# A four-layer graph network on one core: the first layernorm in halves ahead of the adjacency, first tokens over two bank pairs, four units added to x on VectorE, and new due times throughout

## Chip, core and metric

The kernel runs on one core of one Trainium2 chip. The metric is the device time of one execution in microseconds. The time before is the median of three runs, 2805.03 us (2801.18 to 2805.45). A core has five engines with queues of their own: TensorE (PE, with PEld for its weight loads), VectorE (DVE), ScalarE (ACT), GpSimd (POOL) and SyncE (SP), which only issues DMAs. Each engine runs its instructions in the order in which they stand.

## What is computed

Eight samples of 2048 nodes with 128 features pass through four layers, each a layernorm, a relu, graph attention over one adjacency matrix that all share, and an addition to x. Layers 0, 1 and 3 are attention with additive scores (one head); layer 2 has four heads with dot products as scores.

```python
def _L1_gnn_ref(h, adj, W, a):              # layer 0: the same, then elu; layer 3: a second layernorm, residual, elu
    Wh = jnp.einsum('bnf,fo->bno', h, W)
    a_src, a_dst = (a[:F_out], a[F_out:])
    s_src = jnp.einsum('bnf,f->bn', Wh, a_src)
    s_dst = jnp.einsum('bnf,f->bn', Wh, a_dst)
    e = jax.nn.leaky_relu(s_src[:, :, None] + s_dst[:, None, :], negative_slope=LEAKY_SLOPE)
    masked = jnp.where(adj[None, :, :] > 0, e, NEG_BIG)
    attention = jax.nn.softmax(masked, axis=-1)
    return jnp.einsum('bij,bjf->bif', attention, Wh)

def _L2_gnn_ref(input_tensor, adj_matrix):
    x = input_tensor.reshape(B, S, H, F // H)
    scores = jnp.einsum('bihk,bjhk->bhij', x, x)
    scores = jax.nn.leaky_relu(scores, negative_slope=ALPHA)
    scores = jnp.where(adj_matrix[None, None, :, :] == 0, -jnp.inf, scores)
    probs = jax.nn.softmax(scores, axis=-1)
    out = jnp.einsum('bhij,bjhk->bihk', probs, x)
    return out.reshape(B, S, F)

for each layer k:
    h = jnp.maximum(_layernorm(x, axis=-1), 0.0)
    x = x + layer_k(h, adj)
```

## The kernel before

The adjacency is loaded in 16 blocks of 128 rows and turned once into a byte mask, `edge`, that stays in SBUF (`adjacency`, L365). Its symmetry is tested on PE (`symmetry`, L378 and L382), and a slower general path exists for the case that a test fails.

A *unit* is one layer of one sample. The three additive layers are `Gat` units. Their beginning is the layernorm (statistics L448, six small operations L100 to L105, a power on GpSimd L110, L115), the rows of h on ScalarE (L476), and, for each of four quarters, transposes (L504), a copy (L522), the projection (L530), exponentials (L559 to L561) and the rows y (L555). The factors r of all targets are spread over the partitions by PE in three units (L614, L621) and through a row in DRAM in the others. Then come the *tokens*: 32 for a unit, 16 source blocks for each half of the targets. A token is one VectorE operation over 128x1024 (L653, `zg`) and eight matmuls on PE (L662), which the profile shows as 16. When a half is complete its sums are divided (L694, L695), passed through elu where the layer has it, and added to x. In layers 0 and 1 that addition is an accumulating DMA from GpSimd (`plus_a`, L730).

Layer 2 is a `Heads` unit. Its h goes to DRAM in two parts (halves, L803), and is loaded again in other shapes (L817, L823, L828). For each head 16 *beats* follow: four score matmuls on PE (L878), two exponentials on ScalarE (L885), one mask on VectorE (L891) and the weighing with the values on PE (L900). A head ends with a copy, transposes, a division (L920) and an accumulating DMA that adds its columns to x (`gather`, L925).

PSUM has eight banks. `pair` is the name of bank pairs that transposes, projections, scores and the symmetry test take in turn; tokens of place 0 sum in banks 1 to 3. In the first unit alone both halves run together, and place 1 sums in banks 0, 6 and 7, so that only one pair, 4 and 5, is free until that unit ends.

The order of every engine is made while the program is built. `add` records an operation with its engine, an assumed duration, a due time, what it needs, the slots it takes and frees, and `Plan.run` places the operations one after another: of those on an engine that can start within `WINDOW_US` of the first, the one with the lowest due time goes first. The due times come from tables (`TOKENS`, `BEATS`, `LEADS`: start and step by unit) and from `EARLY`, an offset by kind of operation. `order` is then emitted as it stands. The engines' program is fixed by this; on the chip each instruction waits for its inputs alone.

Of the kernel before, what the change touches and what calls it, by code (L numbers as in the profile page):

```python
# [8 lines left out]
F32 = mybir.dt.float32  # L9
# [11 lines left out]
P = 128  # L21
HEADS = 4
# [18 lines left out]
def adj_preln_d4(ctx: ExitStack, tc: tile.TileContext, x, adj, w0, a0, w1, a1, w3, a3,  # L41
# [53 lines left out]
    def moments_begin(stat, name, st):  # L95


        var = stat.tile([P, 4, NB], F32, tag="var", name=f"var{name}")
        total, apart, square, v = (var[:, k, :] for k in range(4))
        nc.vector.tensor_sub(apart, st[:, :, 1], st[:, :, 4])  # L100
        nc.vector.tensor_add(v, st[:, :, 2], st[:, :, 5])
        nc.vector.tensor_add(total, st[:, :, 1], st[:, :, 4])
        nc.vector.scalar_tensor_tensor(square, apart, 0.25, apart, op0=OP.mult, op1=OP.mult)
        nc.vector.tensor_scalar(v, v, 1.0 / C, EPS, op0=OP.mult, op1=OP.add)
        nc.vector.tensor_add(v, v, square)  # L105
        return total, v
# [51 lines left out]
    HURRY_US, WINDOW_US, BEAT_SUMS_US = 372.0, 0.136, 0.86  # L158

    EARLY = dict(front=-36.6, score=230.5, exp=53.6, mask=-103.3, sums=-160.7)  # L160

    SINGLY = (7,)
    PLUS_US, PLUS_LAG_US, GATHER_US, GATHER_LAG_US = 1.0, 5.5, 2.2, 6.5
# [73 lines left out]
    def fast(ctx):  # L237
# [9 lines left out]
        SUMS = ((1, 2, 3), (0, 6, 7))  # L247
        plan = Plan(dict(pair=(4,), sums=(0,), more=(1,), low=0, z=5, zg=3, r=2, h=3, h_t=2, hi=1, lo=1,
# [24 lines left out]
        def load_weights(op):  # L273
# [4 lines left out]
            load(out=a0_sb, in_=a0.rearrange("o (t p) -> p (o t)", p=P))  # L278
            load = nc.gpsimd.dma_start
# [76 lines left out]
        def adjacency(j):  # L356
# [10 lines left out]
            last = add("SP", 2.7, 0.1 * j, load, takes=[tag], lag=3.0)  # L367
            rows_in.append(add("DVE", 1.14, 40.0 + 3.5 * j, edges, [last], frees=[(tag, last)]))

        def symmetry(j):  # L370

            wide = (j + 1) * P
            for k in range(0, wide, 512):
# [12 lines left out]
                due = 130.0 + 9.0 * j  # L386
                last = add("PE", 0.1 + 0.1 * w / P, due, differences, [rows_in[j]], takes=["pair"])
# [23 lines left out]
        def load_x(b, due):  # L411
            def load(op):
                X[b] = big.tile([P, NB, C], F32, tag="x", name="x", bufs=4)
                xv = x[b].rearrange("(n p) c -> p n c", p=P)
                for q in range(4 if b == 0 else 1):
                    sl = slice(q * 4, q * 4 + 4) if b == 0 else slice(0, NB)
                    nc.sync.dma_start(out=X[b][:, sl, :], in_=xv[:, sl, :])

            x_taken[b] = add("SP", 1.5, due, load, takes=["x"], lag=17.0 if b else 5.0)
# [4 lines left out]
        class Unit:  # L424
# [15 lines left out]
            def moments(self, name, part, rows, needs):  # L440
# [17 lines left out]

                last = []
# [5 lines left out]
                return key, add("DVE", 0.09, self.due(part + 0.14), end, last)  # L465

            def rows_made(self, part, step):

                key, last = self.moments("x", 0.0, lambda: X[self.b], [self.after] * 4)
                out = []  # L470
# [14 lines left out]
                for q in range(4):  # L485
                    takes, before = ["h"], []
                    if q == 0 and self.layer != 2:
                        takes, before = ["h", "y"], y_takers[-1:]
                    first = last = add("ACT", 1.54, self.due(part + step * q), lambda op, q=q: rows(op, q),
                                       [last] + before, takes=takes)  # L490
# [18 lines left out]
        class Gat(Unit):  # L509
# [62 lines left out]
            def second(self, ends):  # L572

                key, last = self.moments("h", 0.6, lambda: self.y[:, :, :C], [[e] for e in ends])
# [27 lines left out]
            def spread(self):  # L602
# [4 lines left out]
                if (self.b, self.layer) in ((0, 0), (0, 1), (B - 1, 3)):  # L607
                    for half in range(2):
# [7 lines left out]
                        turned = add("PE", 0.9, self.due(0.95), turn, last, takes=["pair", "r"])  # L616
# [10 lines left out]
                def write(op):  # L627
                    self.row = dram.tile([N], F32, name="row", bufs=4)
                    nc.sync.dma_start(out=self.row.rearrange("(n p) -> p n", p=P), in_=self.cr[:, 1, :])

                self.written = add("SP", 0.5, self.due(0.82 if self.layer == 3 else 0.9), write, last, lag=11.5)

            def targets(self, half, due):
# [10 lines left out]
                self.r_ready[half] = op, op  # L644

            def token(self, a, due, place, last_front, last_back, first, last, gate=None):
# [11 lines left out]
                def back(op):  # L658
                    z = self.z.pop(a)
                    for i in range(HB):  # L660
                        k = i % 3
                        nc.tensor.matmul(ps[:, SUMS[place][i // 3], k * CE:(k + 1) * CE],  # L662
# [9 lines left out]
                        takes=[name] if first else [], frees=[("zg", f)])  # L672
# [9 lines left out]
            def out(self, half, back, place, name, due):  # L682
# [4 lines left out]
                def divided(op):  # L687
# [3 lines left out]
                    for g in range(3):  # L691
                        i0, i1 = g * 3, min(g * 3 + 3, HB)
                        pv = ps[:, SUMS[place][g], :(i1 - i0) * CE].rearrange("p (k c) -> p k c", c=CE)
# [38 lines left out]
                last = taker = add("DVE", 1.75, due - 30, divided, [back], takes=["oa"])  # L732
                last.frees.extend([("pair", 6), ("low", 0)] if place else [(name, self.sums_taker[half])])
                if layer == 1:
                    done.setdefault((b, layer + 1), []).append(
                        add("POOL", PLUS_US, due + 6, plus_a, [last], frees=[("oa", taker)], lag=PLUS_LAG_US))
# [4 lines left out]
                else:  # L741
# [7 lines left out]
                    for k in range(3):  # L749
# [3 lines left out]
                late = due + (10 if layer == 0 else 22)  # L753
                e = add("DVE", 1.14, late, elu_e, [e], frees=[("oe", e_taker)])
                if layer == 0:
                    done.setdefault((b, layer + 1), []).append(
                        add("POOL", PLUS_US, late + 4, plus_a, [last, e], frees=[("oa", taker)], lag=PLUS_LAG_US))
# [12 lines left out]
        class Heads(Unit):  # L770
# [133 lines left out]
            def finish(self, h, weigh, low, due):  # L904
# [19 lines left out]
                def gather(op):  # L924
# [6 lines left out]
                done.setdefault((self.b, 3), []).append(  # L931
                    add("POOL", GATHER_US, due + 5, gather, [last], frees=[("o", turned)], lag=GATHER_LAG_US))
# [6 lines left out]
            (1, 0, 0): (82.8, 3.82), (0, 1, 0): (298.0, 0.56), (0, 1, 1): (-1.8, 0.58),  # L939
            (1, 0, 1): (237.5, 5.12), (2, 0, 0): (716.8, 6.16), (2, 0, 1): (906.2, 4.64),  # L940
            (1, 1, 0): (732.2, 3.64), (1, 1, 1): (825.9, 6.82), (3, 0, 0): (663.1, 5.57),
            (3, 0, 1): (930.0, 5.2), (2, 1, 0): (1062.7, 6.76), (2, 1, 1): (705.4, 6.0),
            (0, 3, 0): (1035.8, 5.99), (0, 3, 1): (1142.1, 4.99), (3, 1, 0): (1367.5, 5.63),
            (4, 0, 0): (905.1, 4.26), (4, 0, 1): (912.9, 5.97), (3, 1, 1): (1359.7, 0.0),
            (1, 3, 0): (1117.7, 6.03), (1, 3, 1): (796.7, 5.75), (4, 1, 0): (778.4, 5.37),
            (4, 1, 1): (1685.2, 3.89), (5, 0, 0): (1293.2, 5.84), (5, 0, 1): (1766.2, 6.15),
            (2, 3, 0): (2097.3, 7.1), (2, 3, 1): (1822.4, 6.83), (5, 1, 0): (1860.6, 4.87),
            (5, 1, 1): (1480.8, 7.43), (3, 3, 0): (1598.7, 4.59), (6, 0, 0): (1737.4, 5.35),
            (6, 0, 1): (2113.6, 6.85), (3, 3, 1): (2672.7, 4.26), (6, 1, 0): (2603.6, 7.7),
            (6, 1, 1): (2772.8, 1.33), (7, 0, 0): (2564.1, 4.71), (7, 0, 1): (2932.1, 6.8),  # L950
            (4, 3, 0): (2517.6, 5.02), (7, 1, 0): (2277.6, 0.32), (7, 1, 1): (2588.8, 7.43),
            (4, 3, 1): (2924.9, 6.32), (5, 3, 0): (2998.9, 5.51), (6, 3, 0): (2609.9, 6.67),
            (5, 3, 1): (2731.2, 7.57), (6, 3, 1): (3009.1, 7.1), (7, 3, 0): (2581.0, 4.89),
            (7, 3, 1): (3032.4, 0.56),
        }
        BEATS = {
            (0, 0): (65.79, 11.57), (0, 1): (-149.43, 13.67), (0, 2): (460.38, 2.51),
            (0, 3): (521.27, 3.93), (1, 0): (151.07, 16.02), (1, 1): (505.63, 8.12),
            (1, 2): (398.27, 6.65), (1, 3): (632.45, 4.8), (2, 0): (616.54, 11.88),
            (2, 1): (827.83, 6.13), (2, 2): (917.3, 2.2), (2, 3): (1137.58, 12.88),  # L960
            (3, 0): (505.03, 9.63), (3, 1): (796.86, 5.93), (3, 2): (1050.45, 2.24),
            (3, 3): (1141.98, 8.73), (4, 0): (1335.0, 23.07), (4, 1): (1518.23, 6.15),
            (4, 2): (1530.27, 6.19), (4, 3): (1810.32, 4.9), (5, 0): (1553.66, 11.16),
            (5, 1): (2021.07, 3.65), (5, 2): (2225.85, 7.65), (5, 3): (2286.21, 0.76),
            (6, 0): (2061.58, 5.82), (6, 1): (2080.76, 0.07), (6, 2): (2097.15, 0.0),
            (6, 3): (2106.74, 13.2), (7, 0): (1522.48, 2.92), (7, 1): (1574.93, 6.28),
            (7, 2): (1813.8, 4.07), (7, 3): (2104.58, 1.02),
        }
        LEADS = {
            (0, 0): 190.15, (1, 0): 14.27, (0, 1): 346.94, (2, 0): 414.97, (1, 1): 500.75,  # L970
            (3, 0): 386.01, (2, 1): 340.86, (0, 3): 529.94, (3, 1): 136.87, (4, 0): 509.55,
            (1, 3): 1755.37, (4, 1): 701.37, (5, 0): 419.44, (2, 3): 1032.06, (5, 1): 76.28,
            (6, 0): 565.92, (3, 3): 513.74, (6, 1): 369.01, (7, 0): 403.81, (4, 3): 213.24,
            (7, 1): 525.14, (5, 3): 302.24, (6, 3): 846.56, (7, 3): 88.27, (0, 2): 390.41,
            (1, 2): 712.99, (2, 2): 419.3, (3, 2): -281.82, (4, 2): -699.34, (5, 2): 257.63,
            (6, 2): -206.25, (7, 2): -140.03,
        }

        def planned():
            weights = add("ACT", 1.0, 0.0, load_weights, lag=4.0)  # L980
            projected[0] = projections(0, 9.0, [weights])
            units[0, 0] = Gat(0, 0, 10.0, 40.0)
            for j in range(NB):
                adjacency(j)
            more = add("POOL", 5.0, 26.0, load_more, lag=4.0)
            projected[1] = projections(1, 50.0, [weights, projected[0]])
# [5 lines left out]
            for n in range(2 * NB):  # L992
                f, b = units[0, 0].token(n % 2 * NB + n // 2, 45.0 + 2.4 * n, n % 2, f, b, n < 2, n >= 2 * NB - 2)
# [231 lines left out]
```

## Time and profile before

| what | us |
|---|---|
| median of three runs | 2805.03 |
| the profiled execution, whole | 2799.68 |
| its span, first to last instruction | 2797.9 |
| PE busy | 2642.8 (94%) |
| VectorE busy | 2510.4 (90%) |
| ScalarE busy | 1713.5 (61%) |
| GpSimd busy | 259.1 (9%) |

The span is the time from the first to the last instruction of the profiled execution; the execution itself took 1.8 us more. "Busy" is time in which an engine works on at least one instruction. A matmul's end is modelled, so PE that is busy may also be waiting within its pipeline. The granted clock is given for PE alone, as a share of full speed; over the whole execution it was 0.989. In a timeline a row has the start, the time from the first to the last of the merged instructions, engine, line, operation, tiles out<-in with their size, the count, and in brackets the engine's idle time before it and what ended it.

### The profile page before, as it was taken

Reading aid. Unit: us, or ns where it says so; the run is one execution under the profiler, and the core shown is the slowest. Engines: PE = TensorE matmul, PEld = TensorE weight load, DVE = VectorE, ACT = ScalarE, POOL = GpSimd, SP = SyncE. Lnnn points to the kernel's source line nnn. Section 1 sums busy time; section 2 is a strip of 40 time slices with the busy share of each in tenths; the row PEclk is TensorE's granted clock in tenths of the full one; section 3 lists DMA queues with packets and bytes.
Section 4 is the critical chain, followed back from the end, with each engine's and each line's share of the span. In section 5 each row is a group of like instructions: output and inputs, shape, how many; then the busy total and the mean of one; then the engine's idle time right before and its main releaser. Section 6 shows DMA issues by size and latency. Waiting matters only on the chain. (4 is left out here: it accounts for less than half of the span.)

```text
span 2797.9 us, 48899 instructions
## 1 busy us (share of the span) xinstructions
PE 2642.8 (94%) x20083; PEld 2030.7 (73%) x20083; DVE 2510.4 (90%) x3309; ACT 1713.5 (61%) x2767; POOL 259.1 (9%) x120
## 2 busy tenths in 40 slices
PE   5999999999998999998999999999999999898987
PEld 4989787767774778886767777765787677564687
DVE  5766799989999999998989998999899999999987
ACT  3432465666668558555667756567676757788541
POOL 1100000002000102000100110000000100001010
PEclk9999999999999999999999999999999999999999
DMA  8003523162134312523232344323226231522010
GB/s 306 24 16 58 102 54 63 43 115 47 49 74 102 56 47 47 96 68 61 49 77 39 61 90 84 61 46 83 46 57 106 46 65 34 110 55 53 12 20 25
DMA packets 258442, 185.20 MB, mean 66 GB/s; under 512 B 187616, under 2 KB 222560, under 8 KB 252064
## 3 DMA queue, kind: packets, MB, share of 16 engines
q1 hardware_dynamic: 186784, 156.46, 23.1%
q0 software_dynamic: 71008, 25.45, 8.7%
q8 instruction: 159, 2.61, 0.4%
q14 instruction: 75, 0.61, 0.1%
q10 hardware_dynamic: 416, 0.07, 0.0%
HBM read 123.03 MB, written 33.73 MB: 56 GB/s over the span
## 5 line engine op out<-in xcount | busy, mean ns | idle before, releaser
L885 ACT ACTIVATE z<-ps,shift 128x1024 f32<-128x1024 f32 x1024 | 1119.4, 1114 | 720.8 <-PE ps L878 709.8
L662 PEld LDWEIGHTS ps<-y,zg 128*128 128x128 f32 x12288 | 1471.0, 193 | 82.8 <-DVE zg L653 29.2
L662 PE MATMUL ps<-y,zg 128*128 128x129 f32 x12288 | 1502.8, 277 | 23.2 <-DVE zg L653 17.3
L891 DVE SCALAR_TENSOR_TENSOR z<-z,edge 128x2048 f32<-128x2048 f32 x512 | 1168.7, 2286 | 73.7 <-ACT z L885 72.5
L653 DVE SCALAR_TENSOR_TENSOR zg<-r,cr,edge 128x1024 f32<-128x1024 f32 x768 | 972.1, 1279 | 113.3 <-PE ps L662 101.7
L878 PE MATMUL ps<-m,s 128*128 128x512 f32 x2048 | 718.9, 437 | 70.7 <-ACT z L885 64.5
L878 PEld LDWEIGHTS ps<-m,s 128*128 128x128 f32 x2048 | 314.4, 191 | 348.6 <-ACT z L885 254.3
L900 PE MATMUL ps<-z,v 128*32 128x512 f32 x4096 | 503.7, 604 | 8.2 <-DVE z L891 8.1
L900 PEld LDWEIGHTS ps<-z,v 128*32 128x32 f32 x4096 | 103.7, 109 | 239.0 <-issue 182.7
L476 ACT ACTIVATE h<-x,nmrx,rstdx 128x128 f32<-128x128 f32 x512 | 210.5, 491 | 53.2 <-DVE nmrx L115 41.1
L110 POOL TENSOR_TENSOR rstdx<-varx,neg_half 128x16 f32<-128x16 f32 x32 | 124.3, 3885 | 644.6 <-DVE varx L105 544.6
L925 POOL DMA_DIRECT2D x<-o x32 | 67.9, 2122 | 785.4 <-DVE o L920 746.7
L448 DVE BATCH_NORM_STATS2 st<-x 128x6 f32<-128x128 f32 x512 | 109.5, 279 | 6.7 <-DMA x<-o 6.7
L530 PEld LDWEIGHTS ps<-rhs,h_t 128*128 128x128 f32 x768 | 100.0, 196 | 15.8 <-ACT h_t L522 7.9
L530 PE MATMUL ps<-rhs,h_t 128*128 128x130 f32 x768 | 106.8, 284 | 4.7 <-ACT h_t L522 4.4
L730 POOL DMA_DIRECT2D x<-oa x32 | 28.9, 902 | 869.6 <-ACT oa L701 220.9
L504 PE MATMUL ps<-ident,h 128*128 128x128 f32 x512 | 80.9, 281 | 5.5 <-ACT y L555 2.8
L504 PEld LDWEIGHTS ps<-ident,h 128*128 128x128 f32 x512 | 63.2, 144 | 26.3 <-ACT h L476 4.6
L522 ACT COPY h_t<-ps 128x512 f32<-128x512 f32 x96 | 55.6, 581 | 40.3 <-PE ps L504 40.2
L695 DVE TENSOR_TENSOR oa<-ps,rs 128x384 f32<-128x384 f32 x144 | 73.9, 513 | 5.1
L555 ACT ACTIVATE y<-ps,y 128x128 f32<-128x128 f32 x256 | 73.0, 369 | 0.0
L701 ACT ACTIVATE oe<-oa 128x1024 f32<-128x1024 f32 x32 | 33.9, 1060 | 59.5 <-DVE oa L720 58.1
(114 smaller groups left out, 810.2 us busy)
## 6 DMA issues: line engine op xcount, KB each, us to landing
s<-halves SPq DMA_DIRECT2D x256, 128.0 KB, 2.7
m<-halves SPq DMA_DIRECT2D x64, 512.0 KB, 6.6
r<-row SPq DMA_DIRECT2D x42, 512.0 KB, 3.7
raw<-in_adj_dram SPq DMA_DIRECT2D x16, 1024.0 KB, 18.2
x<-oa POOLq DMA_DIRECT2D x32, 512.0 KB, 4.7
values<-h SPq DMA_DIRECT2D x32, 256.0 KB, 2.4
halves<-hi SPq DMA_DIRECT2D x128, 64.0 KB, 2.1
halves<-lo SPq DMA_DIRECT2D x128, 64.0 KB, 1.7
```

Of the source, the lines that this page charges most:

```text
L110: nc.gpsimd.tensor_tensor(out=rstd, in0=v, in1=neg_half, op=OP.pow)
L448: nc.vector.bn_stats(out=key["st"][:, n, :], in_=rows()[:, n, :])
L476: nc.scalar.activation(self.h[q][:, k, :], X[self.b][:, n, :], AF.Relu, scale=key["rstd"][:, n:n + 1], bias=key["nmr"][:, n:n + 1])
L504: nc.tensor.transpose(pk[:, k, :], self.h[q][:, k, :], ident)
L530: nc.tensor.matmul(pv[:, k, :C + 2], lhsT=self.h_t[q][:, k * P:(k + 1) * P], rhs=rhs, start=True, stop=True)
L653: nc.vector.scalar_tensor_tensor(z, self.r[half], self.cr[:, 0, jb:jb + 1], edge[:, jb, half * HN:(half + 1) * HN], op0=OP.max, op1=OP.mult)
L662: nc.tensor.matmul(ps[:, SUMS[place][i // 3], k * CE:(k + 1) * CE], lhsT=z[:, i * P:(i + 1) * P], rhs=self.y[:, jb, :], start=(jb == 0 and ...
L695: nc.vector.tensor_mul(key["a"][:, i0:i1, :], pv[:, :, :C], r[:, i0:i1, None].to_broadcast([P, i1 - i0, C]))
L878: nc.tensor.matmul(ps[:, lo + c, :], lhsT=self.S[h, jb // HB][:, at:at + P], rhs=self.M[h][:, (c2 * 2 + c) * 512:(c2 * 2 + c + 1) * 512], ...
L885: nc.scalar.activation(self.z[s][:, c2 * HN:(c2 + 1) * HN], ps[:, lo:lo + 2, :].rearrange("p b t -> p (b t)"), AF.Exp, bias=shift)
L891: nc.vector.scalar_tensor_tensor(self.z[s], self.z[s], 1.0, edge[:, jb, :], op0=OP.mult, op1=OP.mult, accum_out=self.den[:, h, jb:jb + 1])
L900: nc.tensor.matmul(ps[c * HD:(c + 1) * HD, 0, :], lhsT=self.V[h][:, jb, :], rhs=z[:, c * 512:(c + 1) * 512], start=jb == 0, stop=jb == NB - 1,
```

## The change

Seven things are changed.

- The layernorm of the first unit is made in two halves of eight blocks each: statistics, small operations, power and end for half 0, then for half 1 (`first_moments`). The rows of quarters 0 and 1 need the first half only.
- Due times at the start: x of sample 0 and its unit are due before the adjacency's rows; the four loads for layer 3 (`load_more`) wait for the last adjacency row; the projections for layer 1 wait for the first unit's y, and so do the symmetry test's matmuls. One small exponential is issued first on ScalarE.
- `pair` has two pairs at the start, 4 and 6. Place 1 of the first unit takes one of them when its first token comes, with bank 0.
- The first unit's tokens: half 0 runs alone for four, and then the halves alternate.
- Four units, (sample, layer) = (0, 0), (0, 1), (7, 1) and (7, 2), have their addition to x on VectorE (in (7, 2) the last head only). The other additions stay DMAs.
- Assumed durations and lags of loads are altered.
- All of `TOKENS`, `BEATS`, `LEADS`, `EARLY` and two constants have new numbers, so every engine's order is another.

The flags that are `False` leave their branches out of the program.

```diff
-    HURRY_US, WINDOW_US, BEAT_SUMS_US = 372.0, 0.136, 0.86
+    HURRY_US, WINDOW_US, BEAT_SUMS_US = 89.3, 0.131, 0.86
-    EARLY = dict(front=-36.6, score=230.5, exp=53.6, mask=-103.3, sums=-160.7)
+    EARLY = dict(front=-87.0, score=211.3, exp=171.0, mask=-122.3, sums=-168.7)
+    FIRST_ALONE = 4
+    DIRECT, ROWS_TURNED, L1_ACT, L3_DMA, L3_OUT = ((0, 0), (0, 1), (7, 1), (7, 2)), False, False, False, False
...
-        SUMS = ((1, 2, 3), (0, 6, 7))
-        plan = Plan(dict(pair=(4,), sums=(0,), more=(1,), low=0, z=5, zg=3, r=2, h=3, h_t=2, hi=1, lo=1,
+        plan = Plan(dict(pair=(4, 6), sums=(0,), more=(1,), low=0, z=5, zg=3, r=2, h=3, h_t=2, hi=1, lo=1,
...
+            nc.scalar.activation(bad[:, 0:1], shift, AF.Exp)
...
-            last = add("SP", 2.7, 0.1 * j, load, takes=[tag], lag=3.0)
-            rows_in.append(add("DVE", 1.14, 40.0 + 3.5 * j, edges, [last], frees=[(tag, last)]))
+            last = add("SP", 2.5, 5.0 + 0.1 * j, load, takes=[tag], lag=5.5)
+            rows_in.append(add("DVE", 1.14, 20.0 + 3.0 * j, edges, [last], frees=[(tag, last)]))
...
-                last = add("PE", 0.1 + 0.1 * w / P, due, differences, [rows_in[j]], takes=["pair"])
+                last = add("PE", 0.1 + 0.1 * w / P, due, differences, [rows_in[j], *units[0, 0].v_ready], takes=["pair"])
...
+            def first_moments(self):
+                key, ready = {}, []
+                def stats(op, half):
...
+                    for n in range(half * HB, (half + 1) * HB):
+                        nc.vector.bn_stats(out=key["st"][:, n, :], in_=X[0][:, n, :])
+                    sl = slice(half * HB, (half + 1) * HB)
+                    key["total", half], key["v", half] = moments_begin(stat, "x", key["st"][:, sl, :])
+                def power(op, half):
+                    sl = slice(half * HB, (half + 1) * HB)
+                    nc.gpsimd.tensor_tensor(out=key["rstd"][:, sl], in0=key["v", half], in1=neg_half[:, sl], op=OP.pow)
...
+                for half in range(2):
+                    last = add("DVE", 1.9, half, lambda op, half=half: stats(op, half), self.after)
+                    last = add("POOL", 3.4, half, lambda op, half=half: power(op, half), [last])
+                    last = add("DVE", 0.09, half, lambda op, half=half: end(op, half), [last])
+                    ready += [last] * 2
+                return key, ready
...
+            def banks(self, half, place):
+                if not place:
+                    return 1, 2, 3
+                lo = self.sums_taker[half].got["pair"]
+                return 0, lo, lo + 1
...
+                def plus_directly(op):
+                    nc.vector.tensor_add(xs(), xs(), key["a"])
+                def plus(due, needs):
+                    if (b, layer) in DIRECT:
+                        op = add("DVE", 1.14, due, plus_directly, needs, frees=[("oa", taker)])
+                    else:
+                        op = add("POOL", PLUS_US, due, plus_a, needs, frees=[("oa", taker)], lag=PLUS_LAG_US)
+                    done.setdefault((b, layer + 1), []).append(op)
...
+                def gather_directly(op):
+                    xs = X[self.b][:, :, h * HD:(h + 1) * HD]
+                    nc.vector.tensor_add(xs, xs, key["o"].rearrange("p c k d -> p (c k) d"))
+                if (self.b, 2) in DIRECT and h == HEADS - 1:
+                    last = add("DVE", 0.6, due + 5, gather_directly, [last], frees=[("o", turned)])
...
-            (1, 0, 0): (82.8, 3.82), (0, 1, 0): (298.0, 0.56), (0, 1, 1): (-1.8, 0.58),
+            (1, 0, 0): (97.6, 6.88), (0, 1, 0): (73.5, 14.16), (0, 1, 1): (550.6, 7.34),
...
-            (0, 0): 190.15, (1, 0): 14.27, (0, 1): 346.94, (2, 0): 414.97, (1, 1): 500.75,
+            (0, 0): 691.08, (1, 0): 439.88, (0, 1): 835.27, (2, 0): 752.06, (1, 1): 991.07,
...
-            projected[0] = projections(0, 9.0, [weights])
-            units[0, 0] = Gat(0, 0, 10.0, 40.0)
+            projected[0] = projections(0, 3.0, [weights])
+            units[0, 0] = Gat(0, 0, 2.0, 27.0)
...
-            more = add("POOL", 5.0, 26.0, load_more, lag=4.0)
-            projected[1] = projections(1, 50.0, [weights, projected[0]])
+            more = add("POOL", 5.0, 55.0, load_more, [rows_in[NB - 1]], lag=6.0)
+            projected[1] = projections(1, 50.0, [weights, projected[0], *units[0, 0].v_ready])
...
-            for n in range(2 * NB):
-                f, b = units[0, 0].token(n % 2 * NB + n // 2, 45.0 + 2.4 * n, n % 2, f, b, n < 2, n >= 2 * NB - 2)
+            order = sorted(range(2 * NB), key=lambda a: a if a < NB else a - NB + FIRST_ALONE - 0.5)
+            for n, a in enumerate(order):
+                f, b = units[0, 0].token(a, 28.0 + 2.0 * n, a // NB, f, b, a % NB == 0, a % NB == NB - 1)
```

## The prediction

> **What bounds the kernel now.** I read the stretches first (busy time of each engine, cut where the kind of work changes), then the timeline of the start and of the end, then the waits. In the stretches the columns are length, PE, PEld, DVE, ACT, POOL busy (with instruction counts), granted clock, DMA share, GB/s.
>
> ```profile
> 0.00:51.00 51.00, 21.35 (x79) 16.60 (x80) 24.87 (x69) 16.56 (x52) 11.79 (x17) 1.00 0.97 363
> 51.00:318.00 267.00, 246.28 (x2124) 238.37 (x2123) 184.36 (x301) 95.76 (x287) 27.41 (x12) 0.97 0.28 59
> 318.00:2657.00 2339.00, 2258.51 (x16904) 1661.97 (x16904) 2188.45 (x2782) 1555.36 (x2321) 210.15 (x88) 0.99 0.33 63
> 2657.00:2721.00 64.00, 55.94 (x472) 53.92 (x471) 53.84 (x102) 31.69 (x77) 9.78 (x3) 0.96 0.14 22
> 2721.00:2783.00 62.00, 60.76 (x512) 59.80 (x510) 52.03 (x51) 12.04 (x30) 0.00 (x0) 0.96 0.06 18
> 2783.00:2798.00 15.00, 0.00 (x0) 0.00 (x0) 6.86 (x8) 2.11 (x2) 0.00 (x0) 0.66 0.14 40
> ```
>
> PE is the bound nearly everywhere: idle 20.7 us of 267 in the front (graph-attention tokens only), 80.5 of 2339 in the mix of tokens and head beats, 8 of 64 at the last layer change, 1 of 62 in the closing tokens. Outside that lie 51 us at the start, in which PE does not one token, and 15 us of closing VectorE work. So the change can win at the start, in PE's gaps, or not at all. The start:
>
> ```profile
> 19.03 3.85 POOL L110 TENSOR_TENSOR rstdx<-varx,neg_half 128x16 f32<-128x16 f32 x1 [10.07 <-DVE varx L105]
> 24.09 4.71 ACT L476 ACTIVATE h<-x,nmrx,rstdx 128x128 f32<-128x128 f32 x12
> 39.23 2.10 PE L530 MATMUL ps<-rhs,h_t 128*128 128x130 f32 x8 [0.68 <-ACT h_t L522]
> 44.05 2.10 PE L530 MATMUL ps<-rhs,h_t 128*128 128x130 f32 x8 [0.68 <-ACT h_t L522]
> 50.13 1.28 DVE L653 SCALAR_TENSOR_TENSOR zg<-r,cr,edge 128x1024 f32<-128x1024 f32 x1 [4.70 <-ACT r L621]
> 51.91 2.77 PE L662 MATMUL ps<-y,zg 128*128 128x129 f32 x16
> ```
>
> The layernorm of sample 0 is whole: its power starts only at 19.03, because its last two groups of statistics stand on VectorE behind edge rows that wait for the adjacency. Rows are made at 24.09, and the four quarters then go through one pair of PSUM banks, 4.82 us each (39.23 to 44.05), to the first token at 51.91. The front's gaps and the end:
>
> ```profile
> 274.16 2.62 PE L662 MATMUL ps<-y,zg 128*128 128x129 f32 x16 [3.21 <-DVE zg L653]
> 281.72 3.81 PE L662 MATMUL ps<-y,zg 128*128 128x129 f32 x16 [4.09 <-DVE zg L653]
> 312.50 0.75 PE L878 MATMUL ps<-m,s 128*128 128x512 f32 x2 [3.57 <-DMA m<-halves]
> 2662.83 2.08 POOL L925 DMA_DIRECT2D x<-o  x1 [57.63 <-DVE o L920]
> 2671.06 0.87 DVE L448 BATCH_NORM_STATS2 st<-x 128x6 f32<-128x128 f32 x4 [0.42 <-DMA x<-o]
> 2720.49 31.61 PE L662 MATMUL ps<-y,zg 128*128 128x129 f32 x256 [3.34 <-DVE zg L653]
> ```
>
> The last head's add to x is issued by GpSimd at 2662.83, and its readers start at 2671.06: 8.2 us on the chain from the last beat to the last layer's tokens, which PE fills with held-back tokens.
>
> **The start: layernorm in halves, early rows, two pairs.** In the built program SP loads x of sample 1 (1 MB) first, then sample 0 in quarters, then the 16 adjacency rows. The load in front costs between 2.5 us (rows of 1 MB, whose edges start at 21.14 and 23.63) and 5.2 (four times the 1.31 between the first two quarters' statistics, 4.44 and 5.75). So half 0 has landed at 5.75 + 2.5 to 5.2, 8.3 to 11. Then 0.86 of statistics, six small operations (0.6), the power and one operation of 0.17. A power over 8 columns is not in the trace: between 0 and the 3.85 of 16 columns; I take 3.85, the only row of its kind. Rows then begin at 13.7 to 16.4 instead of 24.09. Half 1 waits on VectorE behind three edge rows; before, the third was done at 20.1, so with the load in front at 22.6 to 25.3, unless the four small loads moved behind the adjacency (1.17, 1.15, 0.56, 0.55 us of issue on GpSimd at 5.55 to 8.96) give the rows back about that. ScalarE has, from the ninth row on, to the first r: 8 rows x 0.39, four times 1.45 for exponentials and y, three copies x 0.52, four rows of the next unit (1.6) and the copy of r (1.0), 13.1 us in all. From 17.3 (eight rows and a copy after 13.7) without a wait, or from 22.6 with it: r at 30.4 to 35.7, first token 1.3 later, 31.7 to 37.0 against 51.91. Gain 15 to 20; I take 18. Two pairs make this a ScalarE sum rather than the four 4.82 us round trips. The first eight tokens then alternate with eight edge rows on VectorE (8 x (1.20 + 1.18) = 19 us), beside which PE has eight tokens (14.3) and the next unit's projections (4 x 1.35): cover for both, no loss. If the 25.3 end holds and the power doubles the wait, 10 are left.
>
> The Trainium skill speaks against the order of these loads: "DMA: Bandwidth & Descriptors", section "Queues, rings and completion order", says that each DMA engine consumes descriptors in ring order, so sample 1's megabyte delays sample 0 by all of its time. By the page's bandwidth this would be an estimated 2.4 us, at the lower end of the bounds above.
>
> **The front.** The first tokens run half 0 alone for four, then both halves, the second taking one of the two pairs; total count unchanged. The built order has 107 tokens before the first score in both kernels, so the earlier start moves the first score as a whole (312.5 to about 294). Four adds of layers 0 and 1 of sample 0 go from GpSimd's DMA (0.89 issue, 4.7 to landing) to VectorE (1.14 each, as L716 measures), which has 83 us idle here. That takes some 4 us off each of two chains, under which PE idles 20.7 in all; two of the gaps (274.16, 281.72) come from VectorE and banks, not from the adds. Bounds 0 and -13; I take -4.
>
> One rule bears on every gap. The token after the 4.09 us gap took 3.81 us against 1.95 for its neighbours. "TensorE: Matmul & The Clock Gate", section "What's actually happening", says that an idle window of about 3.4 us halves the clock until a busy one. By it a gap shortened below 3.4 would give back up to 1.9 us more; I don't add it.
>
> **The end.** The last head's add becomes one VectorE operation of about 0.65 (L920, of the same size, takes 0.61): 8.2 - 0.65 = 7.5 us off the chain. The held-back tokens after the last weighing are 50 instead of 56: 6 x 1.79 = 10.7 us less to cover it. So the end is 7.5 us shorter, PE idles about 3 more in it, and the mix takes 10.7 us of tokens: +3. The two adds of layer 1, sample 7, put 2 x 1.14 on VectorE in the mix, which PE bounds: 0 to 2.3, I take 1.
>
> **The mix.** Every due time is new. The work is not: 512 beats, 768 tokens, the same projections. Tokens per 32 beats, counted at the scores of the built orders, ran 47, 38, 42, 23, 45, 63, 39, 36, 54, 40, 26, 45, 35, 32, 16, 22 and now run 48, 37, 43, 27, 32, 58, 43, 43, 31, 47, 44, 49, 26, 37, 20, 24. Where few tokens stand, PE starves: 769 to 898, the stretch of the 23, has PE busy 118.14 of 129 us. The stretches of 23, 16 and 22 become 27, 20 and 24: ten tokens of 1.79 us move into PE's idle time there, while VectorE still pays its 1.2 for each, so up to 10 x 0.59 = 6; I take 5. Bounds of the reshuffle -25 (a third of 80.5 idle gone) and +37 (idle share 3.4% to 5%, between the mix's mean and its worst stretch, 8.4%).
>
> **Sum.** -18 - 4 + 3 + 1 - 5 = -23, taken on the profiled execution: span 2797.9, time 2799.7, to 2777. The runs' median is 2805.0, 5.3 above that execution; on it, 2782.
>
> **Rivals.** (1) The new order starves PE in the mix. The pair of banks between scores and the exponential of z carries the largest wait there:
>
> ```profile
> ACT z L885 <- PE ps L878: 709.8, 604, 7.8
> PEld ps L878 <- ACT z L885: 254.3, 286, 6.5
> ```
>
> If tokens stand less well between scores, PE's idle share of 3.4% grows; from 4.4% (+23) the gain is gone, at 5% the time is 2782 + 37 + 5 = 2824: slower. For it: all 2339 us are reordered; against: the stretches are more even. (2) The megabyte in front and the in-order edges eat the start: -8 instead of -18 gives 2792, still faster. (3) The first score is set by sample 0's store and reload of its halves (3.57 us wait at 312.50), so the start turns into a wait there: -2 of the -23 is left, 2803, no change. (4) The reshuffle also closes gaps: 20 more, 2762. For it: the widest gaps of the mix stand in the token-poor stretches.
>
> **Chances.** Forecast 0.44, (1) 0.15, (2) 0.13, (3) 0.08, (4) 0.20. Faster by over 0.2% (5.6 us, about what a measurement can tell): forecast, (4) and most of (2), 0.75; same, 0.10; slower, 0.15. The range 2752 to 2812 leaves out the far ends of (4) and (1).
>
> **What would show it.** First token of PE near 34 instead of 51.91; first score near 294; PE idle in the mix at 80 plus or minus 20; statistics of the last layer within 1 us of the last head's add; end of the last beat to the end of the span about 133 instead of 141. A first token after 42 makes the start wrong; a mix longer than 2365 makes the forecast wrong.

## The result and the profile after

The changed kernel takes 2776.32 us (median of four runs, 2775.01 to 2778.13) against 2804.66 us for the kernel before beside it: ratio 0.9902, 95% interval 0.9885 to 0.9919. The profiled execution took 2775.01 us, its span 2773.2, so 24.7 less span than before. In the stretches of the changed kernel, cut at the same kinds of work as before (columns as there):

```profile
0.00:36.00 36.00, 16.81 (x73) 12.97 (x73) 20.87 (x74) 18.00 (x57) 15.56 (x19) 1.00 0.96 354
36.00:296.00 260.00, 240.11 (x2107) 232.33 (x2106) 191.02 (x307) 88.92 (x265) 20.31 (x8) 0.97 0.32 75
296.00:2641.00 2345.00, 2269.84 (x17026) 1676.34 (x17025) 2200.14 (x2793) 1563.97 (x2342) 209.95 (x86) 1.00 0.33 63
2641.00:2697.00 56.00, 45.19 (x374) 43.41 (x372) 44.50 (x95) 29.23 (x74) 7.64 (x2) 0.94 0.07 20
2697.00:2759.00 62.00, 60.33 (x512) 59.21 (x512) 52.76 (x53) 12.64 (x32) 0.00 (x0) 0.97 0.07 18
2759.00:2773.00 14.00, 0.00 (x0) 0.00 (x0) 6.55 (x7) 2.11 (x2) 0.00 (x0) 0.60 0.15 42
```

Cut exactly at PE's events, each stretch splits into PE's idle and busy time:

| stretch | before: length (PE idle) | after: length (PE idle) | difference |
|---|---|---|---|
| start to first token | 51.9 (29.7) | 36.9 (19.9) | -15.0 |
| first token to first score | 260.6 (20.7) | 253.6 (19.2) | -7.0 |
| first score to last weighing | 2346.6 (80.5) | 2352.5 (75.2) | +5.9 |
| last weighing to last matmul | 123.8 (9.2) | 115.5 (12.0) | -8.3 |
| rest | 15.0 | 14.7 | -0.3 |

The first score comes 22.0 earlier: 11.3 less idle and 10.7 less busy. Ahead of it both kernels have 107 tokens, but 16 quarters are projected instead of 18. The two (1.06 for eight projection rows and 0.60 for four transposes, 3.3 for both) went into the mix, as did six tokens from behind the last weighing (56 to 50, 1.79 each). So the mix took in 14.0 us of work and grew by only 5.9 (5.3 less idle, the rest pace), and -8.3 behind it is those six tokens (-10.7) with 2.9 us more idle: to a large part one shift, not a loss and a gain. The other 7.4 us of busy time ahead of the first score is pace: matmuls of the same count took less, 2.9 of it in transposes, projections and r, 1.7 in tokens.

The start and the end in the timeline of the changed kernel:

```profile
9.27 1.83 DVE L482 BATCH_NORM_STATS2 st<-x 128x6 f32<-128x128 f32 x8 [4.14 <-DMA x<-in_x_dram]
...
11.92 1.67 POOL L488 TENSOR_TENSOR rstdx<-varx,neg_half 128x8 f32<-128x8 f32 x1 [6.36 <-DVE varx L106]
...
14.57 1.23 DVE L369 TENSOR_SCALAR edge<-raw 128x2048 uint8<-128x2048 int32 x1 [0.15 <-DMA raw<-in_adj_dram]
15.72 0.16 DVE L492 SCALAR_TENSOR_TENSOR nmrx<-varx,rstdx 128x8 f32<-128x8 f32 x1
...
20.68 0.16 DVE L492 SCALAR_TENSOR_TENSOR nmrx<-varx,rstdx 128x8 f32<-128x8 f32 x1
...
36.91 2.05 PE L727 MATMUL ps<-y,zg 128*128 128x129 f32 x16 [0.66 <-DVE zg L718]
...
290.49 1.19 PE L994 MATMUL ps<-m,s 128*128 128x512 f32 x2 [9.43 <-DMA m<-halves]
...
2647.45 0.68 DVE L1049 TENSOR_TENSOR x<-x,o 128x512 f32<-128x512 f32 x1
...
2649.95 0.86 DVE L451 BATCH_NORM_STATS2 st<-x 128x6 f32<-128x128 f32 x4
...
2657.78 9.84 PE L727 MATMUL ps<-y,zg 128*128 128x129 f32 x64 [5.05 <-DVE zg L718]
...
2697.09 3.16 PE L727 MATMUL ps<-y,zg 128*128 128x129 f32 x13 [3.35 <-DVE zg L718]
```

The first statistics start at 9.27, against 4.44 before: sample 1's megabyte in front cost 4.8 us, near the upper of the prediction's bounds (5.2) and twice its estimate of 2.4. All sixteen statistics now stand ahead of the adjacency rows. The power over half the columns took 1.67 us and was done at 13.6, but the operation after it (L492) stands on VectorE behind the first adjacency row, at 14.57, and so ends at 15.9; the second half's stands behind two more rows. The first score now waits 9.43 us for loads, where the kernel before waited 3.57. Behind the last head's add, now 0.68 us on VectorE, the statistics stand behind the divisions of another unit, 1.8 us. The two waits of PE in the last layer, 3.38 and 3.34 before, are 5.05 and 3.35.

### The profile page after: what moved, and what is told of

It is laid out like the page before. It is cut to its first block, busy times and chain, and to the rows that moved or that the text cites. A ratio compares the mean times of both kernels' runs of the same rounds, so it can differ in the third digit from the quotient of the medians.

```text
span 2773.2 us, 48892 instructions
## 1 busy us (share of the span) xinstructions
PE 2632.3 (95%) x20083; PEld 2024.3 (73%) x20083; DVE 2515.8 (91%) x3323; ACT 1714.9 (62%) x2768; POOL 253.5 (9%) x114
## 5 line engine op out<-in xcount | busy, mean ns | idle before, releaser
L718 DVE SCALAR_TENSOR_TENSOR zg<-r,cr,edge 128x1024 f32<-128x1024 f32 x768 | 971.4, 1279 | 119.1 <-PE ps L727 98.3
```

The source lines that it names most:

```text
L718: nc.vector.scalar_tensor_tensor(z, self.r[half], self.cr[:, 0, jb:jb + 1], edge[:, jb, half * HN:(half + 1) * HN], op0=OP.max, op1=OP.mult)
```

## The experiments

All ran in later sets on three chips, each with the kernel before beside it (medians 2800.8 to 2802.1 us), and are set against the changed kernel run again (e5, on the chip of e6, e7 and e8). "Order held" means that the order planned for the changed kernel is kept and only the named operations are moved or issued otherwise; the others are planned anew. The ratio is to the kernel before; "first" and "score" are the starts of the first token and the first score, "last" the time from last weighing to last matmul with PE's idle time.

| run | us | ratio (95%) | first | score | last (idle) |
|---|---|---|---|---|---|
| e5 the changed kernel | 2769.90 | 0.9894 (0.9877-0.9910) | 37.4 | 287.2 | 115.2 (12.0) |
| e1 four adds of sample 0 as DMAs | 2771.09 | 0.9889 (0.9872-0.9905) | 36.2 | 286.8 | 115.6 (12.0) |
| e2 last head's add as DMA | 2773.41 | 0.9900 (0.9883-0.9916) | 37.1 | 287.4 | 119.1 (15.3) |
| e3 head 0's loads first | 2761.43 | 0.9861 (0.9845-0.9878) | 36.2 | 280.0 | 115.5 (12.0) |
| e4 sample 0's x first | 2768.74 | 0.9890 (0.9873-0.9907) | 37.1 | 287.3 | 113.8 (12.4) |
| e6 start reordered | 2769.67 | 0.9898 (0.9881-0.9914) | 33.2 | 288.1 | 113.8 (12.4) |
| e7 moments not in halves | 2767.77 | 0.9890 (0.9873-0.9906) | 38.2 | 286.5 | 113.8 (12.5) |
| e8 one pair at the start | 2794.24 | 0.9978 (0.9968-0.9989) | 64.4 | 310.4 | 116.2 (12.1) |
| e9 changed, old tables | 2835.52 | 1.0119 (1.0102-1.0136) | 34.8 | 296.0 | 115.0 (30.0) |
| e10 before, new tables | 2828.56 | 1.0093 (1.0076-1.0109) | 76.5 | 321.9 | 124.3 (19.6) |
| e11 before, two pairs | 2796.56 | 0.9980 (0.9971-0.9990) | 45.5 | 312.1 | 123.9 (9.2) |
| e12 e3 and the tail reordered | 2761.89 | 0.9857 (0.9840-0.9873) | 37.4 | 281.6 | 115.8 (11.5) |

Times of single runs of one kernel spread over 2 to 8 us, and the first score of the changed kernel came at 290.5 in one execution and at 287.2 in another. So e1, e2, e4, e6 and e7 are not told apart by their times, though e2's four runs (2772.84 to 2774.43) all lie above e5's (2768.99 to 2771.32); what is said of them rests on the stretches of their profiles.

**The adds (e1, e2, order held).**

First the line of e1, then that of e2:

```diff
-                        op = add("DVE", 1.14, due, plus_directly, needs, frees=[("oa", taker)])
+                        op = add("DVE", 1.14, due, plus_a if b == 0 else plus_directly, needs, frees=[("oa", taker)])
...
-                    last = add("DVE", 0.6, due + 5, gather_directly, [last], frees=[("o", turned)])
+                    last = add("DVE", 0.6, due + 5, gather, [last], frees=[("o", turned)])
```

> The four adds of sample 0 (both halves of its layers 0 and 1) are issued as accumulating DMAs on GpSimd again, as in the kernel before; the order of everything else is held. Theory: the chain from sample 0's second layer to the first score is what PE waits for (9.43 us at 290.49), so each late add shows: first score near 296 (5 to 8 later), time 6 above the changed kernel (2776), near 2782. Rival, the low bound of the prediction's step: tokens of sample 1 hide it, first score within 2 of 290.5, time within 2 of 2776.

> Only the add of the last head of sample 7 (ahead of the last layer) goes back to an accumulating DMA; all else is held. Theory: it stands on the chain between the last score and the last layer, issue and landing of a DMA (about 7) in place of 0.68 us of add: PE idle in the last layer 12 -> 18, span from the last mask to the end 132.5 -> 139, time 2782. Rival: the filler tokens hide it, time within 2 of 2776.

e1 came out as its rival: the first score is 0.5 earlier, not 6 later. The timeline of e1 shows why:

```profile
218.28 0.85 POOL L795 DMA_DIRECT2D x<-oa  x1 [28.27 <-DVE oa L760]
219.09 0.86 DVE L451 BATCH_NORM_STATS2 st<-x 128x6 f32<-128x128 f32 x4
...
221.06 0.86 DVE L451 BATCH_NORM_STATS2 st<-x 128x6 f32<-128x128 f32 x4
222.72 0.87 DVE L451 BATCH_NORM_STATS2 st<-x 128x6 f32<-128x128 f32 x4 [0.80 <-DMA x<-oa]
```

The add of the second half is in flight while VectorE takes the statistics of the first half and a token; only 0.80 us of waiting is left, less than the 1.22 that the add itself takes on VectorE (L818 in the changed kernel). The four adds on VectorE brought nothing in this order.

In e2 the end grows by 3.9, of which 3.3 is PE's idle time, half of what was expected:

```profile
2641.55 2.08 POOL L1041 DMA_DIRECT2D x<-o  x1 [53.75 <-DVE o L1036]
2647.84 0.87 DVE L451 BATCH_NORM_STATS2 st<-x 128x6 f32<-128x128 f32 x4 [3.60 <-DMA x<-o]
```

From the issue to its reader it is 6.3 us; in the changed kernel it is 2.5 from the add to the same reader, since the divisions stand between. The DMA lets VectorE do those divisions meanwhile. The price of the DMA is the 3.6 that VectorE waits, not the 8.2 of its chain.

**Head 0's loads (e3, order held).** In both kernels the due times put the loads of head 1 of sample 0 ahead of head 0's, although head 0 is scored first. The edit gives head 0's loads the earlier places among SP's and head 1's the later ones.

```diff
...
         plan.run()
+        (s0, s1, m0, v0), (s2, s3, m1, v1) = (units[0, 2].loads[h] for h in range(2))
+        place = {op: n for n, op in enumerate(plan.order)}
+        for group in ([s0, s1, s2, s3], [m0, m1], [v0, v1]):
+            for op, n in zip(group, sorted(place[op] for op in group)):
+                plan.order[n] = op
```

> Sample 0's heads: the loads of head 0 are issued on SP ahead of those of head 1 (in the changed kernel, as in the one before, head 1's go first, though head 0 is scored first); all else is held. Theory: the 9.43 us wait of the first score is the queue of SP and not the chain behind it: first score at 281 instead of 290.5, time 5 to 9 less, 2767 to 2771. Rival: another wait takes its place directly (exponentials, VectorE), first score at 281 but time within 2 of 2776.

The theory held: score 7.2 earlier, time 8.5 less than e5, the runs apart (2759.33 to 2766.18 against 2768.99 to 2771.32). First SP's issues in e5 and PE's first score (each row of `m` is the load that a score needs), then e3's:

```profile
268.68 1.17 SPq L939 DMA_DIRECT2D m<-halves  x2
...
278.72 1.09 SPq L939 DMA_DIRECT2D m<-halves  x2
...
287.25 1.19 PE L994 MATMUL ps<-m,s 128*128 128x512 f32 x2 [7.83 <-DMA m<-halves]
```

```profile
269.14 1.17 SPq L939 DMA_DIRECT2D m<-halves  x2
...
280.02 0.71 PE L994 MATMUL ps<-m,s 128*128 128x512 f32 x2
```

The first `m` is issued at the same time in both; in e3 it is the one that the score needs, and PE comes to it from its tokens without a wait. The windows from 280 to 300, of e5 and of e3, show the second part of the gain:

```profile
280.00:300.00 20.00, 12.75 (x86) 12.14 (x87) 9.09 (x8) 12.11 (x28) 0.00 (x0) 0.83 0.37 71
```

```profile
280.00:300.00 20.00, 18.94 (x145) 15.49 (x144) 15.79 (x18) 17.45 (x40) 0.41 (x1) 1.00 0.43 85
```

Over these 20 us, the wait included, the mean granted clock is 0.83 in the one and 1.00 in the other, and the first pair of score matmuls takes 1.19 us instead of 0.71. Cut finer, e5's clock is 0.50 from 284.5 to 291.3, 4.1 us of it after the first score has started, by estimate some 2 us lost; in e3 the mix is 1.7 shorter. This agrees with "TensorE: Matmul & The Clock Gate", section "What's actually happening", in the Trainium skill, by which an idle window of about 3.4 us halves the clock.

**The start (e4, e6, e7, order held; e8, e11, planned anew).** `move` puts operations ahead of a named one in the order. e4 has the first two lines; e6 all four, where `after` is the operation that follows the second half's statistics; e7 the third, with the sums, the power and the end made once, over all columns, when the second half's statistics are there.

```diff
+        first, second = sorted(plan.order.index(x_taken[b]) for b in (0, 1))
+        plan.order[first], plan.order[second] = x_taken[0], x_taken[1]
...
+        move(first_powers + first_ends, after)
...
+        move([turned_1, copy_0, copy_1, *sum(first_tokens, [])], units[1, 0].made[0][0])
```

> The load of sample 0's x is issued on SP ahead of sample 1's megabyte; all else is held. Theory: statistics begin near 4.5 instead of 9.27, but VectorE's order puts the end of the first half behind adjacency row 0, which still lands at 14.5: first token within 1 of 36.9, time within 2 of 2776. Rival (the prediction's, that the megabyte in front eats part of the gain of the start): first token near 32, time 5 less.

> At the start alone: sample 0's x loaded first, both ends of its moments ahead of the adjacency rows on VectorE, and the copies of r and the first three tokens ahead of sample 1's first rows on ScalarE and PE; all else held. Theory: what holds the first token is the order on VectorE and ScalarE (the end of the first half waits behind adjacency row 0 at 14.57, the copy of r behind sample 1's rows at 32.99): first token 30 to 31.5, first score as much earlier, time 4 to 6 below the changed kernel. Rival: the adjacency rows, one in 2.5 us, hold the first tokens anyway: first score within 2 of the changed kernel's, time within 2.

> The moments of sample 0's first layernorm made once over all sixteen columns, not in halves, with their end ahead of the adjacency rows on VectorE; all else held. Theory: the halves buy little in the changed kernel's order, because each half's end stands behind adjacency rows: rows of h start at 18.1 instead of 15.9, but nothing waits for a second half: first token within 0 to +2 of 36.9, time within 2. Rival (the prediction's step: the halves bring the first layernorm forward by a power of 3.85): first token at 40 or later, time 3 to 4 more.

e4's first token came out as its theory, to 0.3 us, though statistics began at 7.27 and not near 4.5: small operations that wait for PE stand ahead of them on VectorE. e7 changes two things, no halves and an end ahead of the adjacency rows. Its rows of h start at 17.5 (16.1 in e5), its first token is 0.9 later and the first score no later: against this order the halves are worth no more. It also shows that the order on VectorE, and not the halves, brings rows most of the way from 24.09. In e6 rows of h start at 10.6 and the first token at 33.2, where 30 to 31.5 was expected, because of a wait that the expectation had overlooked:

```profile
31.73 0.17 DVE L116 SCALAR_TENSOR_TENSOR nmrx<-varx,rstdx 128x16 f32<-128x16 f32 x1 [0.53 <-POOL rstdx L111]
31.83 3.67 DVE L722 SCALAR_TENSOR_TENSOR zg<-r,cr,edge 128x1024 f32<-128x1024 f32 x3
...
33.16 7.84 PE L731 MATMUL ps<-y,zg 128*128 128x129 f32 x48 [6.32 <-DVE zg L722]
```

The tokens' operations stand on VectorE behind the end of sample 1's layernorm, at 31.73. But the result is the rival's: the first score did not move. Between first tokens at 33.2 and 38.2 (e4, e5, e6, e7), the ninth token starts at 59.1 to 61.0 in all four. Up to there adjacency rows still come in (the last is turned at 56.9 to 58.9), and in e5 VectorE is busy for 24.5 and PE for 24.8 of the 27 us from 37 to 64. So the first token's time is not what the start is worth. That rows and VectorE's order together hold the ninth token is argued from these numbers; no run took the rows away.

The other suspect was the second pair of banks. The diff is that of e8; e11 has the opposite in the kernel before.

```diff
-        plan = Plan(dict(pair=(4, 6), sums=(0,), more=(1,), low=0, z=5, zg=3, r=2, h=3, h_t=2, hi=1, lo=1,
+        plan = Plan(dict(pair=(4,), sums=(0,), more=(1,), low=0, z=5, zg=3, r=2, h=3, h_t=2, hi=1, lo=1,
...
-                lo = self.sums_taker[half].got["pair"]
-                return 0, lo, lo + 1
+                return 0, 6, 7
...
-                        takes=[name] + ["pair"] * place if first else [], frees=[("zg", f)])
+                        takes=[name] if first else [], frees=[("zg", f)])
...
```

> The plan gets one pair of PSUM banks at the start, as in the kernel before (the second half's sums hold banks 0, 6, 7 from the beginning); all is planned anew, so only the start is read. Theory: from the first row of h to the first token it takes 27.8 as in the kernel before instead of 21.0: first token 42 to 44. Rival: the four quarters are bound by ScalarE (rows, copies, scaling), not by banks: first token within 2 of 36.9.

> The kernel before with only the two pairs of PSUM banks at the start, its own tables. Theory: the second pair is the part that pays at the start: first score 290 to 300 instead of 312.5, time 10 to 20 below 2801. Rival: alone it brings nothing, because the first layernorm, behind the adjacency rows, still gives the first row of h at 24: first score within 3 of 312.5, time within 4 of 2801.

e8 loses 24.3 of the 31 us that e5 is ahead of the kernel before. The expectation was right in kind and short in size: with one pair, all of sample 1's quarters, which the new tables make due first, go ahead of the first token. Its timeline:

```profile
48.71 2.10 PE L566 MATMUL ps<-rhs,h_t 128*128 128x130 f32 x8 [0.67 <-ACT h_t L558]
51.74 1.11 PE L540 MATMUL ps<-ident,h 128*128 128x128 f32 x4 [0.93 <-ACT y L591]
53.53 2.10 PE L566 MATMUL ps<-rhs,h_t 128*128 128x130 f32 x8 [0.68 <-ACT h_t L558]
56.56 2.10 PE L566 MATMUL ps<-rhs,h_t 128*128 128x130 f32 x8 [0.93 <-ACT y L591]
59.59 1.97 PE L650 MATMUL ps<-ident,cr 128*128 128x128 f32 x8 [0.93 <-ACT y L591]
```

Each step waits for ScalarE to empty the one pair (up to 1.6 us idle in the rows from 16.6 on), and the same eight projection rows take 2.10 us here that take 1.06 between tokens. By the first score PE has been busy 262.2 us against 251.4 in e5, with the same counts of every kind of matmul; transposes, projections and r make 9.8 of the 10.8. The rest of the loss is idle time (48.2 against 35.9).

e11 refutes the simple reading that the pair is worth this by itself. In the kernel before it moves the first token from 51.9 to 45.5, but by the 36th token nothing is left of that (136.5 against 135.5), and the score stays at 312.1. The time is 5.5 less than that of the kernel before, between theory and rival; in which stretch is not settled, as no profile of the kernel before was taken beside it.

**Structure and tables (e9, e10).** The diff of e9 puts the five tables and constants of the kernel before into the changed one; e10 is the reverse.

> The changed kernel with the tables of the kernel before (due times, leads, hurry and window), planned anew. Theory: the structure (two pairs, halves, direct adds) carries the gain and the tables little: first score within 8 of 287, time 2770 to 2782. Rival: the retimed tables carry it, since they say which quarters go first and how many tokens are left for the end: time 2790 or more.

> The kernel before with the changed kernel's tables, planned anew. Theory: without the second pair the start gains nothing: first score 305 or later, as with one pair (310.4), time 2790 to 2805. Rival: the tables alone bring more than half of the gain, time 2785 or less.

Both theories failed for the time: each crossing is slower than either kernel. At the start the structure does pay with the old tables: in e9 the first score comes at 296.0, 16.5 ahead of the kernel before, which has the same tables (5.1 of it because two quarters and a token fewer stand before it). The loss comes later. The old tables leave 36 tokens behind the last weighing instead of 50; PE idles 30.0 there instead of 12.0, and the mix, with 15 more tokens (26.9 us), takes 2408.9 us with 94.3 idle against 2350.1 with 75.4. The other 13 us of it are pace, at a mean granted clock of 0.99 against 1.00. So e9's time is the rival's. In e10 the score comes at 321.9, as in e8 and for its reason. The gain in time belongs to neither half alone.

**The tail (e12, order held, with e3's edit).** The four groups of statistics, a token, `begin`, the power and a second token go ahead of three adds of another unit:

```diff
...
+        plan.order[at:stop] = [first, backs[0], *others, backs[1], fronts[0], begin, power, backs[2], fronts[1], backs[3],
+                               *adds[:3], *acts, end, fronts[2], backs[4], *adds[3:], *writes, *fronts[3:]]
...
```

> Two orders together, in the changed kernel: head 0's loads first (2761.4 alone), and in the last layer the statistics of sample 7's layernorm and two tokens ahead of the three adds of the unit before on VectorE; all else held. Theory: the last layer's chain starts 2.6 earlier and the wait of 5.05 of PE there falls to about 3: last mask to end 2 to 3 shorter, time 2758 to 2760. Rival: the tokens that the adds release come late and PE waits later instead: time 2761 or more.

The rival held. From the last head's add to the end of the layernorm it is now 12.3 us instead of 15.5 (e3), but PE's wait of 5.04 there has become two, 4.55 together:

```profile
2642.95 3.92 PE L733 MATMUL ps<-y,zg 128*128 128x129 f32 x32 [1.65 <-DVE zg L724]
2649.76 5.72 PE L733 MATMUL ps<-y,zg 128*128 128x129 f32 x32 [2.90 <-DVE zg L724]
2655.32 0.60 PE L546 MATMUL ps<-ident,h 128*128 128x128 f32 x4
```

The transposes that the layernorm releases stand on PE behind the tokens and the second wait, 19.3 us after the add, before 20.0. So the tail is as long as in e3, and e3's edit is what beats both kernels here: 0.986 of the kernel before in both runs.

## Why the prediction was right, step by step

The forecast was -23 on the profiled execution; its span fell by 24.7. The total was right with several terms wrong against each other.

- *Start, -18, first token near 34.* Measured -15.0 and 36.9, inside the bounds. The power over eight columns was mis-sized (3.85 taken, 1.67 measured), but that changed nothing: rows began at 15.9, within the 13.7 to 16.4, held by the first adjacency row, which the prediction had put ahead of half 1 only. The step "gain of the start" failed in another way: it was counted by the first token, and e4, e6 and e7 show that the first token can move by 5 us and the first score by less than 2.
- *Front, -4 from four adds.* -7.0 was measured, but not from the adds: e1 gives them nothing. It is 1.5 less idle time and 5.5 less busy time: quarters that went into the mix, and pace. That start and front come to -22.0 together, just as forecast, is luck: one term was 3 us too large, the other 3 too small, and for another reason than the one given.
- *The first score "moves as a whole".* It came at 290.5, earlier than 294, and still waited 9.43 us: rival (3), put at 0.08, was half right. Its place was the order of SP's loads, which no step had looked at: e3 takes the wait away for 8.5 us.
- *End, 7.5 off the chain, PE idle 3 more.* The idle time grew by 2.9 as said. The chain's term was mis-sized: e2 prices the add at 3.9, since VectorE uses the wait of the DMA for divisions. Statistics within 1 us of the add: 1.8.
- *Six tokens into the mix, two adds +1, reshuffle -5.* Together +6.7, measured +5.9; PE idle 75.2, in the band of 80 plus or minus 20. The step left out the two quarters, and "reshuffle" as a term apart from the rest is refuted by e9 and e10: the new tables are 66 us faster than the old with this structure (e9 less e5) and 26.5 us slower with the structure before (e10 less its kernel before).
- *Rival (2), the megabyte in front.* The megabyte did cost 4.8 us, but e4 gets 0.3 us of the first token from taking it away. *Rival (1)*, a starved mix, did not come with these tables (3.2% idle). With the old ones (e9) idle is 3.9% of the mix, still under the 4.4% at which the rival had the gain gone.

## What to carry over

Price a wait by what the engine behind it could do meanwhile, not by the length of the chain: an accumulating DMA in flight cost VectorE 0.80 us in one place (e1) and 3.60 in another (e2). Before counting an earlier start, look for the next thing that the stretch waits for, and read the order of the loads there: a swap of two groups on SP's queue brought 8.5 us, more than the halves and the direct adds in any run here. Due times and structure that were fitted to each other can't be judged apart.

## What was not expected of the hardware

- GpSimd's power takes time by its columns, but not always the same: 1.64 and 1.67 us for 8 in the changed kernel, 2.9 to 4.9 for 16. The 3.85 of the prediction was one of these.
- PE keeps its slow pace through a chain of short work: in e8 eight projection rows take 2.10 us from 19.80 to 56.56 with idle gaps of 0.7 to 1.6, against 1.06 between tokens. The clock column reads 1.00 over this stretch, so it does not show it. The same section of "TensorE: Matmul & The Clock Gate" asks for some 3.4 us of sustained activity before the clock is full, which fits the gaps. In e6, with one gap of 0.93 left in a quarter, four transposes take 1.12 at 17.34 and 0.66 from 21.36 on, so fewer gaps go with an earlier full pace; no run varied the gaps alone.
- An accumulating DMA of 128x512 kept GpSimd for 2.08 us of issue (e2), one of 128x1024 only for 0.85 (e1); no run shows why.
